# The first block's FFN chunks in pairs: fp16 products of one chunk last, of the next one first

## The chip, the core and the metric

One core of a Trainium2 chip runs the whole kernel. The metric is the time of one execution on the device in microseconds; a time given for a kernel is the median of its runs. The engines are named as the profile names them: PE is TensorE (matrix products; PEld are its weight loads), ACT is ScalarE, DVE is VectorE, POOL is GpSimd, and SP is the engine that issues nearly all DMA transfers. Each engine works through its own instructions in the order in which the program put them.

## What is computed

The input `x` has 4 sequences of 1024 tokens with 512 channels. It is normalized over the channels, and two branches read the result:

```
xn  = layernorm(x)
xx  = previous_token(xn) - xn
k   = (xn + xx*mix_k) @ Wk.T            # 512 -> 704
r   = (xn + xx*mix_r) @ Wr.T
state_t = state_(t-1) * w + relu(k_t)   # a scan over the tokens
a   = layernorm((state * r) @ Wv.T) * gamma + beta
D   = fp16(gelu(fp16(xn) @ W0.T + bias0))   # 512 -> 2048
E   = fp16(D @ W1.T + bias1)                # 2048 -> 512
out = x + a + E
```

The change is about the second branch, the FFN (`D` and `E`).

## The kernel before

**Blocks and chunks.** The tokens are taken in 8 blocks (`i` = 0 to 7) of 512. Inside a block a loop runs over `n` = 0 to 15, the chunks of the FFN: chunk `n` is 128 of the 2048 hidden units. The work of the attention branch is cut into pieces and spread over the chunks of the same block, and the preparation of the next block's input runs beside it.

**Two products for each weight.** The FFN weights W0 and W1 are held in two parts, a high part as fp32r (a 32-bit format of TensorE) and the rest as fp16. So every step of the FFN has fp32r products and fp16 products, four of each, all 128 x 128 by 128 x 512:

- `up(i, n)` (line 846) makes the hidden units of a chunk: `products(0)` is the fp32r half and `products(1)` the fp16 half of the sum `pd` in a PSUM bank (line 860). Its `after`, called `gelu` in the loop, is two ScalarE instructions: the gelu from `pd` to an fp16 tile (line 874) and a cast of that to fp32r (line 877).
- `down(n, ...)` (line 882) adds the chunk to the four output sums `pe`, one for each 128 tokens (line 886): `p = 0` takes the fp32r gelu and the fp32r part of W1, `p = 1` the fp16 ones.

**Two chunks ahead.** In the loop body of chunk `n`, `hidden(p)` makes the `pd` products of the chunk two further on (`AHEAD = 2`), and `outputs(p)` the `pe` products of chunk `n`. The operands of `pe` come out of a list `waiting`, first in, first out. `LOW_FIRST` and `HIGH_FIRST` say which half opens and which closes a sum.

**Two orders.** In blocks 1 to 7 the chunks go in pairs (`paired`): an even chunk runs `hidden(0)`, `outputs(0)`, the attention piece, and then `hidden(1)`, `outputs(1)`; the odd chunk after it runs `hidden(1)`, `outputs(1)`, `hidden(0)`, `outputs(0)`, and its piece. So sixteen fp16 products lie together. In block 0 every chunk runs `hidden(0)`, `hidden(1)`, `outputs(1)`, `outputs(0)`, and then its piece, if it has one.

**What block 0 does besides.** In block 0 the weights arrive raw and are split on the chip, between the other work:

- `split` (line 198) is one ScalarE instruction for the high part (line 199) and then one VectorE instruction for the low part (line 200), which reads the high one. `split_w0` uses it for W0, `load_w1` for chunk `n + 2` of W1 at the end of every chunk `n`; the parts are also stored to memory for the later blocks (`store_weights`).
- `split_kr` splits weights of the attention branch into three terms, with three instructions of VectorE and two of ScalarE.
- `norm_apply` and `transposed` prepare the input of block 1 on VectorE: 16 transposes in chunks 4 to 9, five of them in chunk 7 (with two `split_kr` and one `split_w0`), five in chunk 9.
- The attention pieces of block 0 are two-pass fp32 products: one `raw_k` or `raw_r` in chunks 1, 3, 5 and 7, `raw_halves` in chunk 9, and `out_piece` in chunks 12 to 15.

**Order.** PE, ACT, DVE and SP run in the order in which the Python program issues their instructions (`tc.manual_schedule`), with semaphores that the framework adds between them. In one chunk of block 0 ScalarE is given: what follows the last attention piece, the gelu and cast of chunk `n + 2`, the jobs of the chunk in `bg[n]` (W0 splits, attention splits), and at last the W1 split of chunk `n + 2`. Tiles rotate through few buffers: four PSUM banks for `pd` and the attention pieces, two buffers for the high and three for the low part of W1.

Of the kernel before, what the change touches and what calls it, by code (L numbers as in the profile page):

```python
# [22 lines left out]
def time_mix_and_gelu_ffn(  # L23
# [39 lines left out]
    NN = N // P  # L63
# [25 lines left out]
    def part(name, dtype=F32R, tag="q", bufs=QS):  # L89
        return wide.tile([P, TB], dtype, tag=tag, name=name, bufs=bufs)  # L90

    def pair(name):
        both = wide.tile([P, 2, TB], F16, tag="q", name=name, bufs=QS)
        return both[:, 0, :], both[:, 1, :]
# [103 lines left out]
    def split(hi, lo, raw):  # L198
        nc.scalar.activation(hi, raw, AF.Copy, scale=WS)
        nc.vector.scalar_tensor_tensor(lo, raw, WS, hi.bitcast(F32), ALU.mult, ALU.subtract)  # L200
# [22 lines left out]
    def load_w0l(i, n):  # L223
        if i > 1 or i == 1 and n >= G:
            w0ls[i, n] = part(f"w0l_{i}_{n}", F16, tag="w0l", bufs=4)
            g, k = divmod(n, G)
            src = w0l_dram[g][:, k].rearrange("p c k -> p (c k)")
            nc.sync.dma_start(w0ls[i, n], src)
# [12 lines left out]
    def load_w1_raw(n):  # L241
        w1_raw[n] = part(f"w1raw_{n}", F32)
        nc.sync.dma_start(w1_raw[n], w1T[n * P : (n + 1) * P, :])

    def as_stored(ap, p):
        return ap.bitcast(F32) if p == 0 else ap

    def load_w1(i, n):
        name = f"w1_{i}_{n}"
        if i == LAST and n >= NN - 2:  # L250
            w1 = [part(f"{name}_0"), pair(f"{name}_1")[0]]
        else:
            w1 = [
                part(f"{name}_0", tag="w1", bufs=2),
                part(f"{name}_1", F16, tag="w1l", bufs=3),
            ]
        if i == 0:
            split(*w1, w1_raw.pop(n))
        for p in range(2):
            sbuf, kept = as_stored(w1[p], p), as_stored(w1_dram[n][p], p)  # L260
            if i == 0:
                stores.append((kept, sbuf))
            else:
                nc.sync.dma_start(sbuf, kept)
        return w1
# [169 lines left out]
    def ffn_input(i):  # L435
        xf = [
            (part(f"xf_{i}_{c}", tag="xf", bufs=4), x16s.pop((i, c))) for c in range(NC)
        ]
        for wide_x, half_x in xf:
            nc.scalar.copy(wide_x, half_x)  # L440
        return xf
# [121 lines left out]
    def finished(*steps):  # L563
        for work in steps:
            for _ in work or ():
                pass
# [269 lines left out]
    def finish(i, s, e16, cols=slice(0, C), adder=nc.vector, queue=nc.sync):  # L836
        z = zs[i][:, s, :]
        b, rows = tokens_of(i, s)
        adder.tensor_tensor(z[:, cols], z[:, cols], e16, ALU.add)
        queue.dma_start(out[b, rows, cols], z[:, cols])  # L840
# [5 lines left out]
    def up(i, n):  # L846
        pd = bank(f"pd_{i}_{n}")
        g, k = divmod(n, G)
        cols = slice(k * P, (k + 1) * P)
        low = w0ls.pop((i, n), None)  # L850
        src = xf

        def weights(c, p):
            if p == 0:
                return w0h[c, g][:, cols]
            return w0l[c, g][:, cols] if low is None else low[:, c * P : (c + 1) * P]

        def products(p, order=HIGH_FIRST):
            for c in range(NC):
                nc.tensor.matmul(  # L860
                    pd,
                    weights(c, p),
                    src[c][p],
                    start=(c == 0 and p == order[0]),
                    stop=(c == NC - 1 and p == order[1]),
                )

        def after():
            if i == 0 or i == LAST and n >= NN - 2:
                d, d16 = part(f"d_{i}_{n}"), pair(f"d16_{i}_{n}")[0]  # L870
            else:
                d = part(f"d_{i}_{n}", tag="d", bufs=2)
                d16 = part(f"d16_{i}_{n}", F16, tag="d16", bufs=2)
            nc.scalar.activation(  # L874
                d16, pd, AF.Gelu, bias=b0_sb[:, n : n + 1], scale=1.0 / WS
            )
            nc.scalar.copy(d, d16)  # L877
            return d, d16

        return products, after  # L880

    def down(
        n, tiles, d, w1, p, order=LOW_FIRST, first=0, end=lambda s: NN, sums=None, cols=slice(0, C)
    ):
        for s in tiles:
            nc.tensor.matmul(  # L886
                (sums or pe)[s],
                d[p][:, s * P : (s + 1) * P],
                w1[p][:, cols],
                start=(n == first and p == order[0]),  # L890
                stop=(n == end(s) - 1 and p == order[1]),
            )
# [34 lines left out]
    def several(fn, *calls):  # L927
        for args in calls:
            fn(*args)

    engines = {e.engine for e in (nc.tensor, nc.vector, nc.scalar, nc.sync)}
    with tc.manual_schedule(engines=engines):
# [17 lines left out]
        waiting = []  # L950
        for n in range(AHEAD):
            products, gelu = up(0, n)
# [8 lines left out]
    with tc.manual_schedule(engines=engines):  # L961
        for i in range(len(blocks)):
            j = i + 1
            tail = 4 if i == LAST else 0
# [107 lines left out]
            for n in range(NN):  # L1072
                ahead = n + AHEAD
                if ahead == NN and j <= LAST:
                    xf = next_xf
                nxt = (i, ahead) if ahead < NN else (j, ahead - NN)
                paired = i > 0 and n < NN - tail
                order = HIGH_FIRST if paired and n % 2 == 0 else LOW_FIRST
                end = lambda s: NN - tail if s in by_columns else NN
                products, gelu = up(*nxt) if nxt[0] <= LAST else (None, None)  # L1080

                def hidden(p):
                    if products:
                        products(p, order if paired else HIGH_FIRST)

                def outputs(p):
                    if n < NN - tail:
                        down(n, range(NS), *operands, p, order, end=end)

                if n < NN - tail:  # L1090
                    operands = waiting.pop(0)
                if not paired:
                    hidden(0)
                    hidden(1)
                elif n % 2 == 0:
                    hidden(0)
                else:
                    hidden(1)
                    outputs(1)
                    hidden(0)  # L1100
                works = [follow() for follow in followers]
                works = [w for w in works if next(w, works) is None]
                several(scaled_now, *early[n])
                if i == 0 or n == out_at[0] or (n > out_at[0] and i < RAW_OUT):
                    finished(*works)
                    works = []
                followers = []
                if behind_works:
                    waiting.append(behind_works.pop()())
                if gelu and not paired:  # L1110
                    d = gelu()
                if ahead + 1 == NN and j <= LAST:
                    next_xf = ffn_input(j)
                if not paired:
                    outputs(1)
                outputs(0)
                if gelu and i > 0:
                    w1 = load_w1(*nxt)
                    if not paired:
                        waiting.append((d, w1))  # L1120
                two_on = (i, ahead + 2) if ahead + 2 < NN else (j, ahead + 2 - NN)
                if two_on[0] <= LAST:
                    load_w0l(*two_on)
                jobs = [
                    lambda s=s: finish(i - 1, s, e16s[s])
                    for s in (2 * n, 2 * n + 1)
                    if s < len(e16s)
                ]
                for work, *args in pieces[n]:
                    followers.append(work(*args))  # L1130
                if i == 0 and ahead + 2 < NN:
                    load_w1_raw(ahead + 2)
                woven(works, jobs + bg[n])
                if i == 0:
                    waiting.append((d, load_w1(*nxt)))
                    for job in behind_w1[n]:
                        job()
                elif paired and n % 2 == 0:
                    hidden(1)
                    outputs(1)  # L1140
                    behind_works.append(lambda gelu=gelu, w1=w1: (gelu(), w1))
                elif paired:
                    waiting.append((gelu(), w1))
                if (i, n) == (1, 6):
                    stores.extend(late_stores)
                store_weights()
# [66 lines left out]
```

## Time and profile before

| | us |
|---|---|
| median of 3 runs | 853.17 |
| lowest, highest | 853.14, 854.71 |
| the profiled execution, time | 853.32 |
| the profiled execution, span from first to last instruction | 851.5 |
| of it: block 0's chunks 2 to 11, about | 44 to 94.5 |

All times below count from the start of the profiled span. The profile's mean granted TensorE clock is 1.00.

How to read its rows: a row of the timeline gives the start, the time from start to end, the engine, the line of the kernel, the operation, output <- inputs, the shapes and the count; in brackets stands how long the engine sat idle before it, and what ended that. Matrix products are pipelined: the ends are modelled, one record (0.38 to 0.39 us for 512 columns) reaches beyond the start of the next, and so the distance between starts is what a product costs, not its record. A short wait of TensorE between two products shows as a longer distance and not as idle time. The names in a row are those of the program with buffer numbers left out; `pd` and `pe` rows marked f32 are the fp32r halves. A merged `pe` row marked f16 x8 is the four fp16 products and the four fp32r ones after them.

### The profile page before, as it was taken

The page shows a single profiled execution, that of the slowest core. Times are in us where ns is not written, and L with a number is a line of the kernel's source. Part 1 is how long each engine was busy: PE and PEld are TensorE (multiplying, and loading weights), DVE is VectorE, ACT ScalarE, POOL GpSimd, SP SyncE. Part 2 cuts the span into 40 slices and gives each one's busy share as a digit, 9 for nine tenths or more (in the row PEclk, how much of TensorE's full clock was granted, in tenths as well). Part 3 has the DMA queues.
Part 4 walks back from the last instruction along what each step waited for, and adds up shares of the span by engine and source line. Part 5 has one row for each costly group of instructions (what it writes and reads, how often), then busy time and mean ns, then how long its engine had stood idle before and what let it go on. Part 6 is the DMA issues. An engine that isn't in the chain of part 4 may idle for free.

```text
span 851.5 us, 11300 instructions
## 1 busy us (share of the span) xinstructions
PE 847.1 (99%) x3756; PEld 592.4 (70%) x3756; DVE 678.1 (80%) x1114; ACT 434.0 (51%) x740; POOL 77.5 (9%) x145
## 2 busy tenths in 40 slices
PE   9999999999999999999999999999999999999998
PEld 8555546776766777766767767767767667776776
DVE  7689898898868978689786888779796897876446
ACT  5866764556444572544634456344653545534422
POOL 1100000000121002000021001100011200200002
PEclk9999999999999999999999999999999999999999
DMA  9976976753485635846458455494455755467513
GB/s 291 342 250 239 297 212 224 229 189 124 149 283 174 210 121 159 288 154 194 161 168 283 146 167 180 160 304 146 154 184 171 267 169 184 125 222 248 168 55 112
DMA packets 121766, 168.30 MB, mean 198 GB/s; under 512 B 21583, under 2 KB 57836, under 8 KB 121708
## 3 DMA queue, kind: packets, MB, share of 16 engines
q1 hardware_dynamic: 121260, 166.91, 60.7%
q8 instruction: 30, 0.49, 0.2%
q10 hardware_dynamic: 448, 0.66, 0.2%
q14 instruction: 28, 0.23, 0.1%
HBM read 142.88 MB, written 24.64 MB: 197 GB/s over the span
## 4 chain that ended last, share of the span: by engine, by line
PE 95%; DVE 3%; ACT 1%; issue 0%; DMA 0%; ACTq 0%
PE pd L860 26%; PE pe L886 26%; PE pa L693 15%; PE oa L790 7%; PE pb L444 7%; PE ob L798 4%; PE ph L722 3%; PE po L749 2%; PE pr L444 2%; PE ob L800 1%; PE pk L444 1%; PE pkr L667 0%; DVE stx L357 0%; DVE wd L287 0%; DMA x<-in_L_attn_x 0%
## 5 line engine op out<-in xcount | busy, mean ns | idle before, releaser
L886 PE MATMUL pe<-w,d 128*128 128x512 f32 (+1 forms) x1008 | 262.0, 388 | 0.1
L860 PE MATMUL pd<-xf,w0h 128*128 128x512 f32 x512 | 151.7, 418 | 0.0
L860 PE MATMUL pd<-x,w0l 128*128 128x512 f16 x512 | 132.2, 381 | 0.0
L874 ACT ACTIVATE d<-pd,late_sb 128x512 f16<-128x512 f32 x128 | 87.1, 681 | 81.5 <-PE pe L886 51.8
L860 PEld LDWEIGHTS pd<-xf,w0h 128*128 128x128 f32 x512 | 96.1, 188 | 29.0 <-issue 4.3
L886 PEld LDWEIGHTS pe<-w,d 128*128 128x128 f32 x504 | 94.7, 188 | 22.1
L706 DVE SCALAR_TENSOR_TENSOR y<-pb,a 128x512 f32<-128x512 f32 x70 | 48.2, 689 | 65.6 <-PE pb L444 55.3
L886 PEld LDWEIGHTS <-d 128*128 128x128 f16 x524 | 50.6, 98 | 60.4 <-issue 1.2
L860 PEld LDWEIGHTS <-w0l 128*128 128x128 f16 x512 | 44.1, 98 | 62.4 <-issue 17.4
L877 ACT CAST d<-d 128x512 fp32r<-128x512 f16 x128 | 79.4, 620 | 10.3 <-PE pe L886 6.3
L383 DVE STREAM_TRANSPOSE xnT<-x 32x512 f32<-32x512 f32 x112 | 78.7, 702 | 2.2
L705 ACT ACTIVATE a<-pa 128x512 f32<-128x512 f32 x70 | 41.8, 597 | 72.5 <-PE pa L693 72.3
L351 POOL TENSOR_SCALAR ry<-mvy 128x1 f32<-128x1 f32 x32 | 18.8, 589 | 421.2 <-DVE mvy L358 421.2
L693 PE MATMUL pa<-hk,kr 128*128 128x512 f32 x140 | 54.5, 389 | 0.0
L693 PE MATMUL pa<-lk,kr 128*128 128x512 f32 x140 | 54.5, 389 | 0.0
L790 PE MATMUL oa<-wv,hg 128*128 128x512 f32 x140 | 54.5, 389 | 0.0
L790 PE MATMUL oa<-wv,lg 128*128 128x512 f32 x140 | 54.5, 389 | 0.0
L693 PE MATMUL pa<-hr,kr 128*128 128x512 f32 x136 | 52.9, 389 | 0.0
L693 PE MATMUL pa<-lr,kr 128*128 128x512 f32 x136 | 52.9, 389 | 0.0
L708 ACT ACTIVATE y<-y 128x512 f32<-128x512 f32 x35 | 22.1, 631 | 52.7 <-DVE y L706 52.7
L805 DVE SCALAR_TENSOR_TENSOR oy<-ob,oa 128x512 f32<-128x512 f32 x28 | 19.3, 689 | 26.2 <-PE ob L800 26.2
L336 ACT CAST hg<-ug 128x512 fp32r<-128x512 f32 x35 | 21.7, 620 | 34.6 <-DVE ug L278 34.5
(167 smaller groups left out, 1387.1 us busy)
## 6 DMA issues: line engine op xcount, KB each, us to landing
kr<-krd SPq DMA_DIRECT2D x207, 256.0 KB, 4.3
w<-w1d SPq DMA_DIRECT2D x112, 256.0 KB, 2.7
w<-w1d SPq DMA_DIRECT2D x112, 128.0 KB, 2.7
w0l<-w0d SPq DMA_DIRECT2D x108, 128.0 KB, 3.5
xres<-in_L_attn_x SPq DMA_DIRECT2D x32, 256.0 KB, 4.7
x<-in_L_attn_x SPq DMA_DIRECT2D x31, 256.0 KB, 4.9
krd<-wt SPq DMA_DIRECT2D x30, 256.0 KB, 2.3
out<-xres SPq DMA_DIRECT2D x28, 256.0 KB, 3.5
```

The source lines that it names most:

```text
L383: nc.vector.transpose(dst[i * Q : (i + 1) * Q, :, :, j, :], src[j * Q : (j + 1) * Q, :, :, i, :],)
L444: return nc.tensor.matmul(dst, w[:, c, :], src, start=(c == 0), stop=(c == NC - 1))
L693: nc.tensor.matmul(pa, w[p][:, c, :], xs[j, c][p], start=(c == 0 and p == 0), stop=(c == NC - 1 and p == 1),)
L705: nc.scalar.activation(a, pa, AF.Copy, scale=1.0 + 1.0 / S)
L706: nc.vector.scalar_tensor_tensor(y, pb, -1.0 / S, a, ALU.mult, ALU.add)
L722: nc.tensor.matmul(pa, w[:, c].rearrange("p two k -> p (two k)"), xs[j, c][p], start=(c == 0 and p == 0), stop=(c == NC - 1 and p == 1),)
L790: nc.tensor.matmul(pa, gs[i, h][p][:, cols], wv[h][p], start=(h == 0 and p == 0), stop=(h == NF - 1 and p == 1),)
L798: nc.tensor.matmul(pb, gs[i, h][2][:, cols], wv[h][2], start=(h == 0), stop=False)
L860: nc.tensor.matmul(pd, weights(c, p), src[c][p], start=(c == 0 and p == order[0]), stop=(c == NC - 1 and p == order[1]),)
L874: nc.scalar.activation(d16, pd, AF.Gelu, bias=b0_sb[:, n : n + 1], scale=1.0 / WS)
L877: nc.scalar.copy(d, d16)
L886: nc.tensor.matmul((sums or pe)[s], d[p][:, s * P : (s + 1) * P], w1[p][:, cols], start=(n == first and p == order[0]), stop=(n == end(s) ...
```

## The change

In block 0 the pairing now begins with chunk 2, the third; chunks 0 and 1 keep the old order. So in chunks 2 to 15 an even chunk runs `hidden(0)`, `outputs(0)`, its piece, `hidden(1)`, `outputs(1)`, and an odd one `hidden(1)`, `outputs(1)`, `hidden(0)`, `outputs(0)`, its piece. The gelu whose `pd` was finished in an even chunk is put into the odd chunk after it; there it is issued right ahead of that odd chunk's own gelu, which stays ahead of the jobs. (In the later blocks the odd chunk's own gelu comes behind the jobs.) The W1 split stays at the end of every chunk. Nothing is computed that was not computed before.

```diff
-                paired = i > 0 and n < NN - tail
+                paired = n >= (2 if i == 0 else 0) and n < NN - tail
                 order = HIGH_FIRST if paired and n % 2 == 0 else LOW_FIRST
...
                 if behind_works:
                     waiting.append(behind_works.pop()())
-                if gelu and not paired:
+                if gelu and (not paired or i == 0 and n % 2):
                     d = gelu()
...
                 woven(works, jobs + bg[n])
                 if i == 0:
-                    waiting.append((d, load_w1(*nxt)))
+                    w1 = load_w1(*nxt)
                     for job in behind_w1[n]:
                         job()
-                elif paired and n % 2 == 0:
+                    if not paired or n % 2:
+                        waiting.append((d, w1))
+                if paired and n % 2 == 0:
                     hidden(1)
                     outputs(1)
                     behind_works.append(lambda gelu=gelu, w1=w1: (gelu(), w1))
-                elif paired:
+                elif paired and i > 0:
                     waiting.append((gelu(), w1))
```

## The prediction

> **What bounds the kernel now.** I read the page first: who is busy, and where the chain of waits that ended last ran.
>
> ```profile
> PE 847.1 (99%) x3756; PEld 592.4 (70%) x3756; DVE 678.1 (80%) x1114; ACT 434.0 (51%) x740; POOL 77.5 (9%) x145
> ...
> PE 95%; DVE 3%; ACT 1%; issue 0%; DMA 0%; ACTq 0%
> ```
>
> TensorE is busy all the time, so a gain can only come from fewer or denser products, and any wait put in front of it is paid in full: no later gap takes it back. By the chain in order of time, its DVE and ACT shares lie in the first 12 us and from 37.4 to 60.4 us, in the first block; from there on it is TensorE alone. It returns to TensorE here:
>
> ```profile
> 59.73 0.70 DVE w L200
> 60.43 0.04 issue
> 60.47 1.94 PE pe L886 x8
> ```
>
> Here TensorE waited for the vector engine: the `pe` products of chunk 5 could not start before DVE had written the fp16 low half of that chunk's W1. So I read the timelines of the three engines from 47 to 97 us. TensorE, chunks 5, 7, 9 and 10:
>
> ```profile
> 59.35 1.04 PE L860 MATMUL pd<-x,w0l 128*128 128x512 f16 x4
> 60.47 1.94 PE L886 MATMUL pe<-w,d 128*128 128x512 f16 x8
> ...
> 70.19 1.04 PE L860 MATMUL pd<-x,w0l 128*128 128x512 f16 x4
> 71.06 1.95 PE L886 MATMUL pe<-w,d 128*128 128x512 f16 x8
> ...
> 79.86 1.08 PE L860 MATMUL pd<-xf,w0h 128*128 128x512 f32 x4
> 80.78 1.04 PE L860 MATMUL pd<-x,w0l 128*128 128x512 f16 x4
> 81.80 1.94 PE L886 MATMUL pe<-w,d 128*128 128x512 f16 x8
> ```
>
> From four fp16 `pd` products to `pe` is 0.87 us at 70.19, but 1.12 at 59.35 and 1.02 at 80.78. The extra 0.25 and 0.15 are waits, however busy the row looks. DVE, columns as above, idle time and its cause at the end of a row:
>
> ```profile
> 59.73 0.69 DVE L200 SCALAR_TENSOR_TENSOR w<-w1raw,w 128x512 f16<-128x512 f32 x1 [0.49 <-ACT w L199]
> 63.75 1.29 DVE L200 SCALAR_TENSOR_TENSOR w0l<-w0raw,w0h 128x512 f16<-128x512 f32 x2 [0.40 <-ACT w0h L199]
> 69.74 0.69 DVE L200 SCALAR_TENSOR_TENSOR w<-w1raw,w 128x512 f16<-128x512 f32 x1
> 73.17 0.69 DVE L200 SCALAR_TENSOR_TENSOR w0l<-w0raw,w0h 128x512 f16<-128x512 f32 x1 [0.41 <-ACT w0h L199]
> 81.06 0.69 DVE L200 SCALAR_TENSOR_TENSOR w<-w1raw,w 128x512 f16<-128x512 f32 x1
> ```
>
> The low halves for chunks 5, 7 and 9 (rows 59.73, 69.74, 81.06) end at 60.42, 70.43 and 81.75; TensorE wants them at 60.22, 71.06 and 81.65. There is no slack. Nor does DVE have any toward ScalarE: the W0 splits that open the jobs of chunks 5 and 7 (63.75, 73.17) wait 0.4 us for ScalarE, and between them and the low half at the chunk's end DVE runs without a break. ScalarE:
>
> ```profile
> 61.87 0.67 ACT L874 ACTIVATE d<-pd,late_sb 128x512 f16<-128x512 f32 x1
> 62.57 0.62 ACT L877 CAST d<-d 128x512 fp32r<-128x512 f16 x1
> 63.10 1.15 ACT L199 ACTIVATE w0h<-w0raw 128x512 fp32r<-128x512 f32 x2
> ...
> 71.26 0.69 ACT L874 ACTIVATE d<-pd,late_sb 128x512 f16<-128x512 f32 x1 [1.17 <-PE pd L860]
> 71.98 0.62 ACT L877 CAST d<-d 128x512 fp32r<-128x512 f16 x1
> 72.51 0.63 ACT L199 ACTIVATE w0h<-w0raw 128x512 fp32r<-128x512 f32 x1
> ```
>
> These are gelu 7 with its cast and the W0 splits queued behind it, then the same for gelu 9, which stood 1.17 us until `pd` 9 was finished while a ready split stood behind it. So PE → gelu → W0 split → DVE → low half of W1 → PE is a loop, tight in chunks 5 to 9.
>
> **What goes: changes of precision.** A bare chunk now takes 3.585 us (88.30, 91.89, 95.47: starts of the same row in chunks 10 to 12). A pair in the later blocks takes 12.56 us (from the chain: 380.81, 393.37, 405.93) and holds 24 more products at 1.81/8 = 0.2266 us; its two chunks are left with 12.56 - 5.44 = 7.12, or 3.56 each. Pairing is worth 0.05 us a pair, 0.35 for all seven. In the walk below a group of four fp32r products counts 0.91 us (half of 1.81) and one of four fp16 products 0.87.
>
> **What moves on TensorE.** H and h are the fp32r and fp16 `pd` groups of the chunk two ahead, O and o the `pe` groups. Today every chunk runs H h o O, piece; an even one will run H O, piece, h o, an odd one h o H O, piece. In odd chunks o comes 0.91 us sooner, and H, on which gelu n+2 now waits in h's place, ends after o.
>
> **What moves on ScalarE.** No instruction is added. Even chunks lose gelu and cast (0.70 + 0.53 us from start to start); odd ones have two sets before their jobs. An even chunk's splits come 1.2 us sooner, but the odd chunk's first W0 split stays behind the same two gelus. Of DVE's work and of SP's loads and stores the order stays; stores follow their splits. The gelu that comes later, of an even chunk m, is wanted by O in m: for chunk 6 about 60.7 against 67.5.
>
> **The walk**, on the clock of the profiled execution. Chunk 2 starts at 44.26 (its fp16 row, 45.17, less 0.91). H O h o end at 47.82, h of chunk 3 at 48.69. Its o needs a low half that DVE ends at 49.16 (row 48.47 + 0.69): it starts at 49.20. With o, H, O and the piece (8 rows, 3.46 us) chunk 3 ends at 55.35, against 54.86 now.
> Chunk 4 ends at 58.91, h of 5 at 59.78. The low half still ends at 60.42, because what ScalarE does before it only changes places; o starts at 60.47, as now, but H is now behind it and ends at 62.25, and O and the piece at 66.62, against 65.70: **0.92 late**.
> Gelu 7 waits for that H. Its record runs about 0.17 past the slot, so it starts near 62.45 instead of 61.87, and the split behind it at 63.68. DVE has no slack to lose: +0.58 for all that follows, and the low half for chunk 7 ends at 71.01.
> Chunk 6 ends at 70.18, h of 7 at 71.05; o starts at 71.06, no wait. H ends at 72.84, so gelu 9 starts at 73.03 instead of 71.26: **+1.77**. W0 split, two three-term splits and five transposes in chunk 7 move with it, and the low half for chunk 9 ends at 83.52.
> Chunk 8 ends at 80.77, h of 9 at 81.64. o waits 1.93 us, to 83.57. H and O end at 86.26; now O of chunk 9 ends at 81.80 + 0.87 + 0.91 = 83.58. **TensorE is 2.68 us late.**
> There the loop ends: chunk 9 has no split ahead of its five transposes, and chunk 11's low half, now ended at 88.74, would end near 90.5, where TensorE asks for it at about 94.5. At the block's end DVE rounds `pe` from 126.24 and TensorE wants the first bank at 129.43; DVE's delay is no larger than TensorE's, so that cover stays.
> What pairing saves before chunk 9 is lost in the waits, which end by DVE's clock; the last three pairs keep 0.14. Sum: 2.68 - 0.14 = **+2.54 us**. The profiled execution took 853.32 us (span 851.5) and would take 855.86; the median of the runs shown is 0.15 lower, which gives 855.7. Measurement tells about 0.2% (1.7 us) from no change; the forecast is 0.3%.
>
> **Clock.** From 44 to 98 us the granted clock is 1.00, with no TensorE wait over 0.25 us; whether one of 1.93 lowers it no row shows, and the sum takes none. The Trainium skill, page "TensorE: Matmul & The Clock Gate", Part 1, says the clock is halved after an idle window of about 3.4 us and restored after a busy one as long. By it 1.93 us is too short; if it fell nonetheless, one such window at half speed would by that page cost some 1.7 us more, an estimate.
>
> **Rivals.** *Precision changes alone*, not slower: 853.17 - 0.35 = 852.8. This needs the low halves by 48.7, 59.3, 70.1 and 80.7, each 0.3 to 1.1 us earlier than now. For it: even chunks' splits come 1.2 us sooner, and DVE idles 0.49, 0.40 and 0.41 us for ScalarE. Against it: those idle times end with the odd chunks' own splits, which do not move ahead.
> *The loop breaks after the first turn*: DVE takes up gelu 9's delay, and chunk 5's 0.92 less two thirds of the 0.35 remain, 853.8 to 854.0. It needs over 1 us of slack in chunk 7, where the row at 73.17 has DVE waiting already.
> *More goes late*: a shared buffer comes free behind a DMA. The waits of the stretch show such steps at 0.6 to 0.8 us (a W1 split behind a store of W1, a weight load behind a DMA); two more of them give 857.3.
>
> **Chances.** The loop as walked 0.64 (855.2 to 856.2), broken loop 0.11, precision alone 0.08, more 0.17. Range 853.8 to 857.3, which leaves out the precision case and about half of the last. Faster by over 0.2%: 0.03, since 0.35 us is all that TensorE could save; within 0.2% (up to 854.9): 0.17; slower: 0.80.
>
> **What will show it.** Waits before `pe` of chunks 5 and 9, of about 0.7 and 1.9 us, behind DVE's line 200; gelu 7 near 62.5 and gelu 9 near 73.0, each waiting for `pd`; the low halves for chunks 7 and 9 ending near 71.0 and 83.5; a shift that stays near 2.6 us from chunk 10 on. Low halves for 5, 7 and 9 at their old times would prove the loop wrong.

## The result: 2.9 us slower, and the profile after

The changed kernel takes 856.45 us (median of 9 runs, 855.88 to 857.37), the kernel before 853.53 us (9 runs, 853.14 to 854.71): a ratio of 1.0033, 95% interval 1.0025 to 1.0042.

The profiled execution took 857.30 us with a span of 855.5, which is 4.0 more than the 851.5 of before. Not all of that is the change. The first row of `pr` products, ahead of everything that was changed, starts at 21.00 us here and at 19.72 before. No instruction ahead of this row was changed, all kernels here have it between 19.72 and 21.08, and the nine runs of the kernel before alone lie up to 1.57 us apart; so the 1.28 us is taken for scatter, and spans and starts are compared from this row on: what is left is +2.69 us at the first `pd` row in block 1's chunks, and it stays so to the end. A time of the changed kernel less 1.28 is on the clock of the prediction.

TensorE, fp16 rows of chunks 3, 5, 7 and 9 (`pd`, then `pe`; of chunk 3 the `pe` row alone):

```profile
50.49 1.02 PE L886 MATMUL pe<-w,d 128*128 128x512 f16 x4 [0.36 <-DVE w L200]
...
60.23 1.03 PE L860 MATMUL pd<-x,w0l 128*128 128x512 f16 x4
61.75 1.02 PE L886 MATMUL pe<-w,d 128*128 128x512 f16 x4 [0.49 <-DVE w L200]
...
71.49 1.03 PE L860 MATMUL pd<-x,w0l 128*128 128x512 f16 x4
72.38 1.02 PE L886 MATMUL pe<-w,d 128*128 128x512 f16 x4
...
82.08 1.03 PE L860 MATMUL pd<-x,w0l 128*128 128x512 f16 x4
84.91 1.02 PE L886 MATMUL pe<-w,d 128*128 128x512 f16 x4 [1.81 <-DVE w L200]
```

From the start of `pd` to that of `pe` it is 0.87 us where nothing waits; here it is 1.39 in chunk 3 (`pd` starts at 49.10), then 1.52, 0.89 and 2.83. The brackets count only idle time after the modelled end of a record, so 0.36, 0.49 and 1.81 stand for waits of 0.52, 0.65 and 1.96. With the 0.02 of chunk 7 they come to 3.15 us, against 0.40 before (0.25 and 0.15): 2.75 more, and TensorE is 2.74 late at chunk 10. In chunks 5, 7 and 9 `pe` starts 0.06 us after a row of line 200 on DVE ends (the rows at 61.00, 71.63 and 84.16):

```profile
61.00 0.69 DVE L200 SCALAR_TENSOR_TENSOR w<-w1raw,w 128x512 f16<-128x512 f32 x1 [0.49 <-ACT w L199]
65.64 1.29 DVE L200 SCALAR_TENSOR_TENSOR w0l<-w0raw,w0h 128x512 f16<-128x512 f32 x2 [1.56 <-ACT w0h L199]
71.63 0.69 DVE L200 SCALAR_TENSOR_TENSOR w<-w1raw,w 128x512 f16<-128x512 f32 x1
76.26 0.69 DVE L200 SCALAR_TENSOR_TENSOR w0l<-w0raw,w0h 128x512 f16<-128x512 f32 x1 [1.62 <-ACT w0h L199]
84.16 0.69 DVE L200 SCALAR_TENSOR_TENSOR w<-w1raw,w 128x512 f16<-128x512 f32 x1
```

DVE, in turn, now waits 1.56 and 1.62 us for the W0 splits of ScalarE (0.40 and 0.41 before). ScalarE, gelus 7 and 9:

```profile
63.74 0.69 ACT L874 ACTIVATE d<-pd,late_sb 128x512 f16<-128x512 f32 x1 [0.50 <-PE pd L860]
...
74.36 0.69 ACT L874 ACTIVATE d<-pd,late_sb 128x512 f16<-128x512 f32 x1 [2.20 <-PE pd L860]
```

The chain of waits goes once around, from TensorE over ScalarE (gelu 9, then the W0 split behind it) and DVE back to TensorE:

```profile
73.40 0.94 PE pd L860 x4
...
74.36 0.70 ACT d L874
...
75.61 0.63 ACT w0h L199
...
76.26 0.69 DVE w0l L200
```

It stays on DVE until line 200 at 84.16 and returns to `pe` at 84.91.

### The profile page after: what moved, and what is told of

The parts are those of the page before. It is cut to its first block, busy times and chain, and to the rows that moved or that the text cites. A ratio compares the mean times of both kernels' runs of the same rounds, so it can differ in the third digit from the quotient of the medians.

```text
span 855.5 us, 11298 instructions
## 1 busy us (share of the span) xinstructions
PE 848.6 (99%) x3756; PEld 595.0 (70%) x3756; DVE 678.0 (79%) x1114; ACT 433.9 (51%) x740; POOL 78.1 (9%) x145
## 4 chain that ended last, share of the span: by engine, by line
PE 95%; DVE 3%; ACT 1%; issue 1%; DMA 0%; ACTq 0%
PE pd L860 26%; PE pe L886 25%; PE pa L693 15%; PE oa L790 7%; PE pb L444 7%; PE ob L798 4%; PE ph L722 3%; PE po L749 2%; PE pk L444 2%; PE ob L800 1%; PE pr L444 1%; DVE wd L287 0%; PE pkr L667 0%; DVE w L200 0%; DMA x<-in_L_attn_x 0%
```

## The experiments

All are variants of the changed kernel; each is compared with the kernel before. Ahead of the details, their shifts against the kernel before, in us, each trace counted from its own first `pr` row: at the first `pd` row of chunk 10, at the first `pd` row of block 1, and at the end of the span; then the difference of the medians of timed runs (8 to 11 of each variant and 21 to 31 of the kernel before, on the same chip; 9 and 9 for the change), which holds the scatter of the start as well. The intervals of the ratios reach about 0.1%, some 0.8 us, to either side, so smaller differences rest on one trace of each kernel. How well two traces agree from the first `pr` row on shows in the fifth row: that kernel is unchanged up to chunk 10, and differs there by 0.01 us.

| kernel | chunk 10 | block 1 | end | median |
|---|---|---|---|---|
| the change | +2.74 | +2.69 | +2.7 | +2.9 |
| own gelu behind the jobs | +0.02 | -0.04 | 0.0 | +0.1 |
| pairs in chunks 2 to 5 | +0.92 | +0.93 | +1.0 | +1.1 |
| pairs in chunks 6 to 9 | +2.15 | +2.16 | +2.1 | +2.0 |
| pairs from chunk 10 | -0.01 | -0.11 | 0.0 | +0.2 |
| transposes behind the W1 split | +1.09 | +1.01 | +1.9 | +2.4 |
| W1 split first | -0.50 | -0.55 | +0.2 | +0.3 |
| W1 split first, no pairs in block 0 | -0.39 | -0.38 | -0.4 | -0.5 |
| W1 split first, own gelu behind in all odd chunks | -0.50 | -0.27 | -0.2 | -0.5 |
| W1 split first, own gelu behind from chunk 11 | -0.50 | -0.53 | -0.5 | -0.5 |

**The order of products, or the place of the gelu?** The theory is the loop of the prediction. The rival says that the loss comes from TensorE alone, which asks for the low half of W1 0.91 us sooner. The first kernel keeps TensorE's order and moves the odd chunk's own gelu behind the jobs and the W1 split, in block 0 as in the later blocks:

```diff
-                if gelu and (not paired or i == 0 and n % 2):
+                if gelu and not paired:
                     d = gelu()
...
-                    if not paired or n % 2:
+                    if not paired:
                         waiting.append((d, w1))
...
-                elif paired and i > 0:
+                elif paired:
                     waiting.append((gelu(), w1))
```

> The changed kernel, but in the odd chunks of the first block the chunk's own gelu is issued behind the jobs and the W1 split, as in the later blocks. The order of products on TensorE is that of the change. Theory (loop): the wait of gelu 7 and gelu 9 for the fp32r pd products no longer holds back the W0 splits, so the low half for chunk 9 no longer ends later than in the kernel before (81.75 on its clock; expected 80 to 82), the waits before pe of chunks 5 and 9 (0.7 and 1.9 us) shrink to under 0.3 us, and the loss against the kernel before falls from 2.7 us to about 0 (-0.3 to +0.5). Rival (order of products alone): the loss comes from asking for the fp16 W1 half 0.91 us sooner in every odd chunk, the place of the gelu plays no part: still 2.0 to 2.9 us.

Measured: ratio to the kernel before 1.000 (0.9991 to 1.0009), +0.02 us at chunk 10. The waits of chunks 5 and 9 are gone, and only that of chunk 3 is left. That row, and DVE's low half for chunk 9:

```profile
49.48 1.02 PE L886 MATMUL pe<-w,d 128*128 128x512 f16 x4 [0.36 <-DVE w L200]
...
79.59 0.69 DVE L200 SCALAR_TENSOR_TENSOR w<-w1raw,w 128x512 f16<-128x512 f32 x1
```

Its first `pr` row starts at 19.99, so 0.27 comes off for the clock of before; the low half for chunk 9 (79.59 + 0.69) ends at 80.01, against 81.75 before and 83.57 with the change. TensorE makes the same products in the same order; the place of one gelu in each odd chunk decides on 2.7 us.

**One turn of the loop, and the other alone.** Two kernels have pairs in a part of block 0:

```diff
-                paired = n >= (2 if i == 0 else 0) and n < NN - tail
+                paired = (i > 0 or 2 <= n < 6) and n < NN - tail
```

> The changed kernel with pairs in chunks 2 to 5 of the first block alone; chunks 6 to 15 keep the order of the kernel before. Theory (loop): one turn, the 0.9 us of chunk 5, less 0.1 for two pairs; gelu 7 near 0.6 us late, but in the old order the pe products of chunk 7 and 9 have 0.9 us more, so no new wait: +0.7 to +1.0 us. Rival (order alone, the same price for each pair with a wait): also about +0.9 us. It fixes the first term of the sum.

Measured: +0.92 us at chunk 10, ratio 1.0010 (1.0001 to 1.0020). The second has `6 <= n < 10`:

> The changed kernel with pairs in chunks 6 to 9 alone. Theory (loop): even without any loss in chunk 5, gelu 9 waits for the fp32r pd group of chunk 7 and starts 0.9 to 1.2 us later than in the kernel before; the low half for chunk 9 ends as much later; to that comes the 0.91 us of the group H behind it: +1.8 to +2.1 us. Rival (order alone): the low half for chunk 9 ends when it did, and the loss is the 0.91 us, with the wait of chunk 9 near 0.9 us: +0.8 to +1.0 us.

Measured: +2.15 us, ratio 1.0024 (1.0015 to 1.0033). Its rows of gelu 9 and of the `pe` of chunks 7 and 9 (0.36 comes off for the clock of before):

```profile
72.85 0.69 ACT L874 ACTIVATE d<-pd,late_sb 128x512 f16<-128x512 f32 x1 [2.44 <-PE pd L860]
```
```profile
70.86 1.02 PE L886 MATMUL pe<-w,d 128*128 128x512 f16 x4 [0.21 <-DVE w L200]
...
83.39 1.02 PE L886 MATMUL pe<-w,d 128*128 128x512 f16 x4 [1.80 <-DVE w L200]
```

Gelu 9 starts 1.23 us later than before (72.49 against 71.26), and `pe` of chunk 9 also by 1.23 (83.03 against 81.80); the fp32r group now behind it adds 0.91: 2.14. The rival's 0.8 to 1.0 is out. The parts do not add up to the whole, 0.92 + 2.15 = 3.07 against 2.74, as a loop would have it: what chunk 5 loses makes TensorE ask later in chunk 7, where the low half then comes with a wait of 0.02 us. Without that loss chunk 7 waits 0.37 us (its `pd` starts at 69.62, its `pe` at 70.86), which accounts for the 0.33. The expectation had left this wait out, and 2.15 lies just above its range.

**Pairs where there is slack.** With `10 <= n < 16` nothing should wait:

> The changed kernel with pairs in chunks 10 to 15 alone. Both theories: no wait in front of pe, since the low halves of chunks 11, 13 and 15 are 4 us and more ahead; what remains is the saving of three pairs, 0.05 us each: -0.15 us (-0.3 to +0.2), too small for the times and only to be read in the trace. A loss of 0.5 us or more would show a cost of pairing beside the waits of chunks 3 to 9.

Measured: -0.11 us at block 1 in the trace and nothing in the times (ratio 0.9999, 0.9989 to 1.0008). Where no low half is short, pairing costs nothing by itself.

**Cutting the loop on DVE.** Gelus and products stay as in the change; the transposes of chunks 5 and 7 go behind the W1 split of their chunk:

```diff
-                put(5, turn, 1, 5)
+                behind_w1[5].append(lambda: turn(1, 5))
-                put(7, turn, 5, 10)
+                behind_w1[7].append(lambda: turn(5, 10))
```

> The changed kernel, with the four transposes of chunk 5 and the five of chunk 7 issued behind the W1 split of their chunk instead of ahead of it. Order of products and place of the gelus are those of the change. Theory (loop through DVE's queue): gelu 7 and gelu 9 still start late, as in the changed kernel (0.6 and 1.8 us), but the low halves for chunks 7 and 9 end 2.9 and 3.6 us sooner than there, so the wait of chunk 9 (1.8 us) is gone and that of chunk 5 stays: +0.7 to +0.9 us against the kernel before. Rival (TensorE is held by the gelus themselves or by the order of products): the wait of chunk 9 stays, +2.5 us or more.

Measured: the wait in chunk 9 is gone while gelu 9 is as late as with the change (74.42; the clocks of the two differ by 0.08):

```profile
83.01 1.03 PE L886 MATMUL pe<-w,d 128*128 128x512 f16 x4
```
```profile
74.42 0.69 ACT L874 ACTIVATE d<-pd,late_sb 128x512 f16<-128x512 f32 x1 [2.18 <-PE pd L860]
```

So it is the low half on DVE that holds TensorE there, not the gelu itself. The low halves came 2.4 and 3.2 us sooner, not 2.9 and 3.6, as they now wait 0.49 us for ScalarE. But the total was missed: +1.0 at block 1, +1.9 at the end, ratio 1.0030 (1.0019 to 1.0040). Two losses came in elsewhere. The first, 0.33 us, is in chunk 9: before, the first four `pkr` products start together (83.68 to 83.70), here two start at 85.80 and 85.81 and the other two at 86.14 and 86.15. DVE's product that reads the sum `pr` of chunk 7 runs from 85.40 to 86.09, now behind the transposes. That it frees the bank for the later two fits to 0.05 us, but is not shown: no run tries it by itself. The second lies at the start of block 1, where four `pe` products take 1.77 us (131.82 to 133.59) instead of 0.92, and is taken up below.

**W1 split first.** In chunks 1, 3, 5, 7 and 9 the W1 split goes ahead of the jobs, on both engines:

```diff
+                first = i == 0 and n % 2 and n < 10
+                if first:
+                    w1 = load_w1(*nxt)
                 woven(works, jobs + bg[n])
                 if i == 0:
-                    w1 = load_w1(*nxt)
+                    if not first:
+                        w1 = load_w1(*nxt)
```

> The changed kernel, with the W1 split of chunks 1, 3, 5, 7 and 9 issued ahead of the other jobs of its chunk, on ScalarE and on VectorE. Theory: the low halves for chunks 3, 5, 7 and 9 are ready 1 us and more before TensorE asks for them, no wait is left in front of pe, not even the 0.25 and 0.15 us of the kernel before, and the saving of pairing (0.05 us a pair, 0.35 in all) shows at last: -0.5 to -0.8 us against the kernel before. Rival (W1 split early only moves the wait: the W0 and attention splits behind it now come late for pd): no gain, 0 or slower.

The control has the same edit and no pairs in block 0 (`paired = i > 0 and n < NN - tail`):

> The kernel before, its order of products and gelus unchanged, with the W1 split of chunks 1, 3, 5, 7 and 9 ahead of the other jobs. Theory: only the waits of 0.25 us (chunk 5) and 0.15 us (chunk 9) go: -0.4 us. The distance of this kernel to the one with pairs and early W1 splits is what pairing is worth when nothing waits: 0.2 to 0.4 us. Rival: pairing is worth nothing by itself, both end at the same time.

Measured: the control gains what was expected, -0.39 us at chunk 10 and -0.4 at the end, ratio 0.9994 (0.9986 to 1.0003). With pairs it is -0.55 at block 1, with no wait left in front of `pe` in block 0. So pairing is worth 0.17 us there, a little less than the 0.2 to 0.4 expected. But at the end it is +0.2, ratio 1.0003 (0.9994 to 1.0012). That is the rival's number, for a reason that neither side named: up to block 1 TensorE shows no wait for an operand of `pd`. The gain and a little more, 0.73 us, is lost at one place, the first four `pe` products of block 1, which must wait for DVE to round the sums of block 0 out of the same banks. TensorE and DVE, and last DVE's row of chunk 13 in the kernel before:

```profile
130.03 1.80 PE L886 MATMUL pe<-w,d 128*128 128x512 f32 x4
131.68 0.40 PE L693 MATMUL pa<-hk,kr 128*128 128x512 f32 x1
```
```profile
114.11 0.69 DVE L200 SCALAR_TENSOR_TENSOR w<-w1raw,w 128x512 f16<-128x512 f32 x1 [2.04 <-ACT w L199]
...
128.81 2.48 DVE L833 SCALAR_TENSOR_TENSOR e<-pe,b_sb 128x512 f16<-128x512 f32 x4
```
```profile
111.61 0.69 DVE L200 SCALAR_TENSOR_TENSOR w<-w1raw,w 128x512 f16<-128x512 f32 x1 [0.73 <-ACT w L199]
```

Four products take 1.65 us instead of 0.92. The third and fourth start at 130.75 and 131.34, 0.06 us after the third and fourth rounding end (130.69 and 131.28). DVE begins to round 1.2 us before TensorE wants the first bank, against 3.2 before, since in chunk 13 it waited 2.04 us for the W1 split (0.73 before), which stands on ScalarE behind both gelus. Two kernels test that. In the first, the own gelu goes behind the jobs in all odd chunks:

> Pairs from chunk 2 on, the W1 split of chunks 1, 3, 5, 7 and 9 ahead of the jobs, and the odd chunk's own gelu behind the jobs in every odd chunk of the first block. Counted from the first pr product. Theory (the kernel with W1 splits first lost 0.75 us at the start of block 1, because the second gelu of chunk 13 held back the W1 split there, DVE waited 2.04 us for it instead of 0.73, and so rounded pe too late): the W1 split of chunk 15 no longer waits, no wait in front of the first pe products of block 1, and the 0.5 us that the first block gains last to the end: -0.4 to -0.7 us against the kernel before. Rival (the loss at the start of block 1 comes from the W1 splits that were moved up): the wait of about 0.75 us stays, +0.2 us in all.

In the second only in chunks 11, 13 and 15:

```diff
-                if gelu and (not paired or i == 0 and n % 2):
+                if gelu and (not paired or i == 0 and n % 2 and n < 10):
...
-                    if not paired or n % 2:
+                    if not paired or n % 2 and n < 10:
...
-                elif paired and i > 0:
+                elif paired and (i > 0 or n > 10):
```

> As the kernel with pairs from chunk 2 on and the W1 split of chunks 1, 3, 5, 7 and 9 ahead of the jobs; the odd chunk's own gelu goes behind the jobs only in chunks 11, 13 and 15. Theory: the places of gelus 5 to 11 do not matter once the W1 split goes first, those of chunks 11 to 15 alone decide on the wait at the start of block 1: it is gone, -0.4 to -0.7 us against the kernel before. Rival (delay carried over from chunks 3 to 9): the wait of 0.75 us stays, +0.2 us.

Measured: the wait at the start of block 1 is gone in both; 2.0 and 2.1 us between the first rounding and the first bank wanted are enough. The DVE row of chunk 13 and the `pe` row of block 1 of the second kernel:

```profile
112.35 0.69 DVE L200 SCALAR_TENSOR_TENSOR w<-w1raw,w 128x512 f16<-128x512 f32 x1 [0.73 <-ACT w L199]
```
```profile
129.15 1.09 PE L886 MATMUL pe<-w,d 128*128 128x512 f32 x4
```

The second keeps its gain to the end, -0.5 us; ratio 0.9992 (0.9983 to 1.0001). Counted from the first `pr` row it is the fastest of all traces, and its interval still holds 1. The first ends at -0.2 (ratio 0.9994, 0.9985 to 1.0003), short of what was expected: it loses 0.25 us in chunk 14, ahead of and in its `po` products. The first weight load of `po` starts at 113.24, after 0.44 us idle that the trace puts down to line 874 on ScalarE: chunk 13's own gelu, now behind the jobs, runs there from 112.53 to 113.20. In the second kernel that gelu runs from 112.22 to 112.89, the load starts at 112.94 and nothing is lost. So a gelu that stands last can hold TensorE as well. That `po` needs a bank which this gelu must read first, and why it is 0.3 us later in the first kernel, is not shown.

## Why the prediction was right

The forecast was 855.7 us and +2.54; the trace has +2.69, and the medians differ by 2.92. The absolute 856.45 lies above the 855.2 to 856.2 that the prediction named for the loop as walked, but these stand on 853.17, the median of three runs; with all nine runs the kernel before has 853.53, and the same shifts (+2.0 to +3.0) give 855.6 to 856.6. The steps, on the clock of before (the changed trace less 1.28):

| step | predicted | measured |
|---|---|---|
| `pe` of chunk 5 starts | 60.47 | 60.47 |
| gelu 7 starts | 62.45 | 62.46 |
| low half for chunk 7 ends | 71.01 | 71.04 |
| gelu 9 starts | 73.03 | 73.08 |
| low half for chunk 9 ends | 83.52 | 83.57 |
| `pe` of chunk 9 starts | 83.57 | 83.63 |
| TensorE late at chunk 10 | 2.68 | 2.74 |
| saved by the last three pairs | 0.14 | 0.05 |

- *The loop* is shown, at each of its links: with the gelu behind the splits the loss is gone; without DVE's transposes in the way the wait in chunk 9 is gone although the gelu is late; pairs in chunks 2 to 5 alone cost the walk's first term (0.92), and pairs in chunks 6 to 9 alone the delay of gelu 9 and one fp32r group (1.23 + 0.91). The wait of chunk 3, 0.52 us, was in the walk too (`pe` at 49.20; measured 49.21).
- *The rival "the loop breaks after the first turn"* is what pairs in chunks 2 to 5 show, +0.92 us, and it needs the old order in chunks 7 and 9. *"Precision alone"* had its condition right: with early low halves, nothing waits in block 0. Its price was mis-sized: 0.05 us a pair, 0.35 in all, was read off the later blocks. The kernels with W1 split first, with and without pairs, differ by 0.17 us at block 1 (-0.55 and -0.38), 0.02 a pair. *"More goes late"* did not happen; the trace shows no DMA wait in front of TensorE.
- *The end of the block* was wrong, and by luck cost nothing. The prediction said that DVE would be no later than TensorE there. DVE rounds at 130.72 - 1.28 = 129.44, 3.20 us later than before, TensorE is 2.69 later: the cover shrank by half a microsecond, through the two gelus of chunk 13, a place that the walk passed over. Since TensorE was 2.69 us late itself, no wait came of it. In the kernels with the W1 split first and with the transposes behind it the cover fell to 1.2 and 1.1 us, and that step was the bill: 0.73 and 0.85 us. With pairs from chunk 10 alone 2.0 us of it were left, and no wait came.
- *The chain before* was read a little too short: from 60 us on it is not TensorE alone, since its last 6 us (from 845.20) go over DVE. Nothing in the sum rests on that.
- *The clock.* After the wait of 1.96 us in chunk 9 the four fp32r `pd` products take 1.12 us from start to start (85.58 to 86.70), and 1.11 in chunk 7 where nothing waited (73.05 to 74.16): no slower clock, and the granted clock stays 1.00. That agrees with the Trainium skill, page "TensorE: Matmul & The Clock Gate", Part 1, by which it takes about 3.4 us without work to slow the clock.
- The rest between 2.69 and 2.92 us is not told apart from scatter: the interval of the ratio stands for +2.1 to +3.6 us, and the code ahead of the change scatters by 1.36 us between the profiles here.

## What to carry to other kernels

When products on the bounding engine are put into another order, each consumer of a moved result gets another time too: look at what is queued behind that consumer on its engine, and follow it until it comes back to the bounding engine. Here a reordering worth 0.17 us cost 2.7 because one in-order engine waited for a result that now came 1.8 us later, with ready work behind it that a second engine had no slack for. An operand that is needed soonest should be made first, and a step that waits for the bounding engine should stand behind the work that is ready, but not so late that the bounding engine comes to wait for it; and covers at block ends have to be counted again for each engine, since a delay elsewhere can hide that they are gone.

## What the runs showed that was not expected

The first 20 us differ between profiles though the change touches no instruction there. In the changed kernel's profile the first 18 products of `pk` (128 columns) take 3.38 us, before 2.25:

```profile
7.47 3.38 PE L444 MATMUL pk<-xk,wk 128*128 128x128 f32 x18
```
```profile
6.93 2.25 PE L444 MATMUL pk<-xk,wk 128*128 128x128 f32 x18
```

The granted clock of both profiles is 1.00 in that stretch, so the clock record does not tell them apart, and what does stays open. By the first `pr` row 1.28 us of it are left, about half of the effect studied here.
